# A four-layer graph network on one core: layer 2 back to plain tile order, and one layer turned on TensorE

## The chip, the core and the metric

The kernel runs on one core of a Trainium2 chip. Its engines work side by side and are ordered by semaphores: TensorE (PE) multiplies and transposes into the eight PSUM banks, VectorE (DVE) and ScalarE (ACT) do the elementwise work and empty the banks, GpSimd (POOL) takes small elementwise jobs, SyncE (SP) issues every DMA. The metric is the device time of one execution in microseconds (us).

## The reference, cut to what matters

A batch of 64 graphs of 256 nodes with 256 features goes through four layers, each with a normalisation without weights in front and a residual sum behind it:

```
h = relu(layernorm(x)); x = x + layer0(h, adj)   # attention, 8 heads: softmax over masked scores
h = relu(layernorm(x)); x = x + layer1(h, adj)   # additive attention, softmax over axis 1, elu
h = relu(layernorm(x)); x = x + layer2(h, adj)   # gated graph network, 3 rounds
h = relu(layernorm(x)); x = x + layer3(h, adj)   # additive attention, 4 heads
```

Layer 2 repeats three times, with the state `h` starting as its input:

```
m = h @ weight[i]; aggr = A.T @ m               # A = (adj != 0)
gi = aggr @ w_ih.T + b_ih; gh = h @ w_hh.T + b_hh
r, z = sigmoid(gi_r + gh_r), sigmoid(gi_z + gh_z)
n = tanh(gi_n + r * gh_n); h = (1 - z) * n + z * h
```

Layer 3 needs, per head, softmax over the keys of `leaky_relu(s_src + s_dst)` where the adjacency is 1, times the projected features.

## The kernel before, in words

Two graphs make a pair; 32 pairs pass through the four layers. A pair is a tile `x` of 128 partitions by four token groups (`t` 0 to 3, `T` = 4) of 256 features. Work tiles (`w4`, 29 slots of 128 x 1024 fp32) are shared by all pairs in flight; at most five pairs are (`x` has five slots).

*The plan.* Nothing is issued where the code stands. `add` (lines 73 to 109) records each task with its engine or engines (`forms`), its assumed duration and what it reads and writes. `order` (111 to 184) then simulates all engines and picks, again and again, the task and form that can begin first; ties go to the lower key, which is the pair's rank times `PERIOD` plus an offset per layer: `ON_PE` for TensorE, `ON_SP` for SyncE, `OTHERS` for the rest (lines 60 to 63). `MARGIN` is added in front of a DMA issue, `BACK` is a handicap for an engine of a task that could go elsewhere, and `RANKS` (1242) sets when the weights of layers 1 to 3 are prepared. Each engine, and SyncE as the queue of all DMAs, then runs its instructions in that fixed order.

*Normalisation* (`norm_relu_T`, 495 to 572). VectorE takes the statistics (L502, L504), GpSimd the power -0.5 of the variance (L516, L517). In layers 0, 1 and 3 VectorE scales each token group (L537), TensorE transposes the tile in eight 128 x 128 blocks (L555), and the two banks are emptied with the Relu (L567). Layer 2 needs its input in both forms, token by token (`xn`) and turned (`hT`). There the shift is worked out first (L523), ScalarE applies scale, shift and Relu (L532), and in all pairs but the last the tile is turned through DRAM.

*Turning through DRAM* (`through_dram`, 613 to 623). VectorE transposes 32 x 32 blocks, one DMA writes the tile to DRAM (L616), four read it back so that whole blocks change places (L619): five issues on SyncE. `turn` (625) does this for the attention tiles of layers 0 and 3 (L627), `turn_chunks` (630) for layer 2, in two half-tile transposes (L636). A tile from `turn_chunks` is *mixed*: node, then feature half, then token group, so that neighbours of one chunk lie eight elements apart. `chunk` (575) reads one chunk as weights, `wide` (582) a feature half as a moving operand.

*Layer 2* (`layer2`, 913 to 1154). Before the change `by_dma` (491) says that three tiles per pair go through DRAM: the normalised one and the states after rounds 0 and 1. Because the first is mixed, `woven` is set: the messages `aT` (evicted by L322, at 971) and the states `u` hold the four token groups of one node side by side, so chunks of them lie four elements apart. In rounds 0 and 1 the gates are products with the weights as the stationary and `hT` or `aT` as the moving operand, 512 columns wide (L988). In round 2 the tiles are the stationary operand, in chunks (L1084), for 512 columns (two gates) and for 256 (the new state). `messages` (943) splits the state into three bf16 parts, two of them remainders: the first subtraction (L946) also puts the token order right, the second is L951; 24 bf16 products per round (L965) multiply them by the adjacency mask.

*Layer 3* (`layer3`, 1156 to 1240). Prelu (L1191), mask and row minimum (`lowered`, L661), Exp (L669), the turn through DRAM (L627, L616, L619), products with the turned tile (L1213), transposes back (L1228), division (L1235), sum (L1240). In the last pair the normalisation in front is done in two halves (`fine`).

Of the kernel before, what the change touches and what calls it, by code (L numbers as in the profile page):

```python
# [16 lines left out]
P = 128  # L17
# [5 lines left out]
class Buf:  # L23


    def __init__(self, tag, tiles):
        self.tag, self.tiles, self.slot, self.parts = tag, tiles, None, {}
        self.fine = False
        self.woven = False
        self.mixed = False  # L30
# [9 lines left out]
class Plan:  # L40
# [15 lines left out]
    SLOW, MARGIN = 1.3, 0.6  # L56
    BACK = {"DVE": 1, "POOL": 1.1}


    PERIOD, REST = 133.7, 0  # L60
    ON_PE = (940, -967, 1371, -841)
    ON_SP = (1493, 2561, -1056, -1316)
    OTHERS = (1067, -773, -952, 397)
# [124 lines left out]
def tile_adj_preln_d4(  # L188
# [121 lines left out]
    def pool(n):  # L310
        return 0.16 + n / 460.0
# [14 lines left out]
    def either(do):  # L326

        return [(G, pool(N2), lambda: do(nc.gpsimd), True), (V, dve(N2), lambda: do(nc.vector), True)]
# [162 lines left out]
    def by_dma(what, p):  # L491

        return p < B // 2 - 1 and what in (2, (2, 0), (2, 1))

    def norm_relu_T(xt, p, tokens=False):
# [15 lines left out]
        xn, mixed, fine = w4(), by_dma(plan.layer, p), plan.layer == 3 and p == B // 2 - 1  # L511
        shift = tokens or mixed
        for ts in (slice(0, 2), slice(2, 4)) if fine else (slice(0, T),):
# [7 lines left out]
            if shift:  # L521
                add(
                    (V, 0.17, lambda: nc.vector.scalar_tensor_tensor(  # L523
                        rs()[:, 1, :], mv()[:, :, 0], -1.0, rs()[:, 0, :], ALU.mult, ALU.mult)),
                    reads=[mv], writes=[rs],
                )
        for g in range(2):

            def scaled(g=g):
                for t in (2 * g, 2 * g + 1):  # L530
                    if shift:
                        nc.scalar.activation(  # L532
                            tok(xn())[:, t, :], tok(xt())[:, t, :], AF.Relu,
                            bias=rs()[:, 1, t : t + 1], scale=rs()[:, 0, t : t + 1],
                        )
                    else:
                        nc.vector.tensor_scalar(  # L537
                            tok(xn())[:, t, :], tok(xt())[:, t, :], mv()[:, t, 0:1], rs()[:, 0, t : t + 1],
                            ALU.subtract, ALU.mult,
                        )  # L540

            add((A, 0.95, scaled) if shift else (V, 0.7, scaled, True), reads=[(xt, g), (mv, g), (rs, g)], writes=[(xn, g)])
        hT = w4()
        if mixed:
            turn_chunks(xn, "(t k b j)", hT)
            return (at, hT, xn) if tokens else (at, hT)
# [27 lines left out]

    def chunk(hT, k, t):
        if hT.mixed:
            return hT().rearrange("p (n x) -> p x n", x=2 * T)[:, T * k + t]
        if hT.woven:
            return tok(hT(), N2)[:, k].rearrange("p (n t) -> p t n", t=T)[:, t]
        return tok(hT(), N2)[:, k, t * P : (t + 1) * P]  # L580

    def wide(hT, k):

        if hT.mixed:
            return hT().rearrange("p (n k t) -> p k n t", k=2, t=T)[:, k]
        return tok(hT(), N2)[:, k]
# [43 lines left out]
    def turn_chunks(src, order, dst):  # L630

        e = w4()

        def blocks():
            for k in range(2):
                nc.vector.transpose(  # L636
                    e().rearrange("p (b i k t) -> p k b t i", b=4, i=32, k=2)[:, k],
                    src().rearrange(f"p {order} -> p k b t j", b=4, j=32, k=2)[:, k],
                )

        add((V, 2 * dve(N2), blocks), reads=[src], writes=[e])
        through_dram(e, dst)
        dst.mixed = True
# [13 lines left out]
    FUSED = 0.36  # L657
# [5 lines left out]
    def exp_rows(e, mn, zs, z0):  # L663


        def do():
            for r in range(4):
                row = rows_of(e())[:, r]
                nc.scalar.activation(  # L669
                    row, row, AF.Exp, bias=mn()[:, r : r + 1], scale=-1.0, accum_out=zs()[:, z0(r) : z0(r) + 1]  # L670
# [4 lines left out]
    def layer0(xt, p):  # L675
# [11 lines left out]
        for w, dst, nm in ((wq_sb, qT, "q"), (wk_sb, kT, "k")):  # L687
            for o in range(2):
                ps = bank()

                def product(w=w, o=o, ps=ps):
                    for k in range(2):
# [3 lines left out]
                by_node = lambda ap, hT=hT: ap.rearrange("p (t n) -> p n t", t=T) if hT.mixed else ap  # L696
                add(
                    evict(
                        N2, lambda dst=dst, o=o, f=by_node: f(tok(dst(), N2)[:, o, :]),
                        lambda ps=ps, hT=hT: tok(ps(), T) if hT.mixed else ps(),  # L700
                    ),
                    reads=[ps], writes=[(dst, o)],
                )
        for g in range(2):
            ps = bank()
            add((PE, 2.0 if hT.mixed else 1.74, lambda ps=ps, g=g: graph_mm(ps, hT, wv_sb, g)), reads=[hT, (QKV, 2)], writes=[ps], claims=[v])
# [3 lines left out]
        for g in range(2):  # L710
# [29 lines left out]
            for e, eT, mn in zip(es, pT, mns):  # L740
# [12 lines left out]
                for i in range(2):  # L753
# [3 lines left out]
                            (A, 2 * act(N, 1), lambda f=divided, rows=rows: f(nc.scalar.mul, rows)),  # L757
# [54 lines left out]
    def layer1(xt, p):  # L812
# [8 lines left out]
        for t in range(T):  # L821
# [6 lines left out]
            add((PE, 0.96 if hT.mixed else 0.89, product), reads=[hT, W1], writes=[ps], claims=[wh, f12])  # L828
# [29 lines left out]
        for g in range(2):  # L858
# [9 lines left out]
            def exp(g=g):  # L868
# [5 lines left out]
            add((V, 0.18, lambda two=two: nc.vector.reciprocal(rz()[:, two], zs()[:, two])), reads=[(zs, g)], writes=[(rz, g)])  # L874
            add(
                (V, dve(N2), lambda two=two: nc.vector.tensor_tensor(
# [422 lines left out]
```

## Time and profile before

| | us |
|---|---|
| median of 3 runs (3769.93 to 3773.58) | 3770.68 |
| profiled execution | 3770.94 |
| its span, first to last instruction | 3769.1 |
| TensorE busy | 3679.7 |
| VectorE busy | 3093.9 |
| ScalarE busy | 2521.8 |
| GpSimd busy | 594.1 |

A line of the profile names an engine, an operation, the tiles (out <- in), shapes and a count, and then durations. "Busy" is the union of the instructions' intervals. Matmuls overlap in their last part, so the spacing of their starts is their cost, and a busy TensorE may still hold short waits. `PEld` is the loading of a stationary operand, which runs beside the products. `w <- turn` is the way back from DRAM.

### The profile page before, as it was taken

How to read it: one execution, taken by the hardware profiler on the slowest of the kernel's cores; microseconds unless marked ns; L12 is line 12 of the kernel's file. 1: busy time of each engine (PE TensorE's matmuls, PEld its weight loads, DVE VectorE, ACT ScalarE, POOL GpSimd, SP SyncE). 2: the span in 40 equal slices, each digit the busy share in tenths (PEclk: the TensorE clock that was granted, in tenths of full speed). 3: DMA queues.
4: the chain of work that ended last, by engine and by line, in shares of the span. 5: the costliest groups of instructions: out<-in, count | busy, mean ns of one | idle time of the engine just before them, and what ended most of it. 6: DMA issues, size and time to landing. Idle time of an engine off the chain costs nothing.

```text
span 3769.1 us, 56446 instructions
## 1 busy us (share of the span) xinstructions
PE 3679.7 (98%) x17097; PEld 2308.8 (61%) x17097; DVE 3093.9 (82%) x7982; ACT 2521.8 (67%) x6756; POOL 594.1 (16%) x543
## 2 busy tenths in 40 slices
PE   7999999999999999999999999999999999999996
PEld 4556665666666666666666666666666666666663
DVE  7678779888888888888888888888888888888765
ACT  7776477776667776667776667776667776667544
POOL 2001111111112111111111111111121011121100
PEclk9999999999999999999999999999999999999997
DMA  8664367755566655566655566655666655666324
GB/s 235 171 196 129 105 195 199 201 163 169 164 184 201 183 170 169 162 191 197 188 166 168 162 191 199 187 166 165 170 188 196 188 165 165 171 194 185 115 79 129
DMA packets 469167, 651.88 MB, mean 173 GB/s; under 512 B 47744, under 2 KB 395264, under 8 KB 468864
## 3 DMA queue, kind: packets, MB, share of 16 engines
q1 hardware_dynamic: 468864, 648.28, 59.0%
q8 instruction: 137, 2.24, 0.2%
q14 instruction: 166, 1.36, 0.1%
HBM read 380.91 MB, written 267.19 MB: 172 GB/s over the span
## 4 chain that ended last, share of the span: by engine, by line
PE 29%; DVE 21%; ACT 14%; DMA 5%; issue 2%; SPq 2%; POOL 1%; POOLq 0%; DVEq 0%; ACTq 0%
PE ps L988 11%; ACT w L669 5%; PE ps L1084 5%; DMA w<-turn 5%; DVE st L502 3%; DVE w L537 3%; PE ps L1166 2%; PE ps L965 2%; ACT w L1191 2%; PE ps L592 2%; DVE w L627 2%; DVE w L636 2%; DVE w L1146 1%; SPq L619 1%; PE ps L720 1%
## 5 line engine op out<-in xcount | busy, mean ns | idle before, releaser
L669 ACT ACTIVATE w<-w,mx 128x256 f32<-128x256 f32 x1536 | 762.5, 508 | 36.0 <-DVE mx L661 35.8
L988 PE MATMUL ps<-w,whhT 128*128 128x512 f32 x1536 | 728.6, 601 | 3.8 <-DMA w<-turn 3.6
L988 PE MATMUL ps<-w,giT 128*128 128x512 f32 x1536 | 708.9, 593 | 0.2 <-ACT w L322 0.2
L322 ACT COPY w<-ps 128x512 f32<-128x512 f32 x518 | 386.3, 765 | 344.6 <-PE ps L592 151.8
L627 DVE STREAM_TRANSPOSE w<-w 128x1024 f32<-128x1024 f32 x384 | 473.1, 1238 | 104.3 <-ACT w L669 55.3
L988 PEld LDWEIGHTS ps<-w,giT 128*128 128x128 f32 x1536 | 288.9, 190 | 351.2 <-issue 331.9
L988 PEld LDWEIGHTS ps<-w,whhT 128*128 128x128 f32 x1536 | 276.8, 191 | 301.9 <-issue 282.6
L661 DVE CUSTOM_DVE_ANT_0 w<-ps,mask 128x256 f32<-128x256 f32 x1024 | 368.6, 417 | 44.1 <-PE ps L720 42.8
L751 ACT ACTIVATE w<-w,rz 128x256 f32<-128x256 f32 x910 | 387.9, 505 | 5.0 <-DVE rz L744 3.4
L1084 PE MATMUL ps<-whhT,w 128*128 128x512 f32 (+1 forms) x1024 | 375.6, 504 | 0.1
L1084 PE MATMUL ps<-giT,w 128*128 128x512 f32 (+1 forms) x1024 | 364.3, 494 | 0.0
L1084 PEld LDWEIGHTS ps<-giT,w 128*128 128x128 f32 x1024 | 281.7, 312 | 74.5 <-issue 5.1
L1084 PEld LDWEIGHTS ps<-whhT,w 128*128 128x128 f32 x1024 | 274.5, 317 | 64.2 <-issue 14.8
L669 ACT ACTIVATION_READ_ACCUMULATOR w<-w,mx 128x1 f32 x1536 | 309.4, 201 | 0.0
L1031 POOL TENSOR_TENSOR w<-w,w 128x512 f32<-128x512 f32 x91 | 121.7, 1338 | 1168.8 <-ACT w L1026 1077.8
L965 PE MATMUL ps<-mask,w 128*128 128x256 bf16 x2304 | 272.0, 274 | 4.0 <-DVE mask L917 2.9
L965 PEld LDWEIGHTS <-w 128*128 128x128 bf16 x2304 | 231.3, 108 | 70.9 <-issue 45.7
L661 DVE CUSTOM_DVE_ANT_0 w<-w,mask 128x256 f32<-128x256 f32 x512 | 201.5, 425 | 29.7 <-ACT w L1191 29.7
L1191 ACT ACTIVATE w<-w,f 128x256 f32<-128x256 f32 x512 | 219.2, 511 | 0.0
L1117 ACT ACTIVATE w<-w 128x512 f32<-128x512 f32 x128 | 80.2, 627 | 192.0 <-DVE w L1113 190.9
L636 DVE STREAM_TRANSPOSE w<-w 128x512 f32<-128x512 f32 x186 | 197.3, 1122 | 10.6 <-ACT w L532 10.6
L537 DVE TENSOR_SCALAR w<-x,mv,rs 128x256 f32<-128x256 f32 x384 | 165.7, 484 | 47.9 <-POOL rs L517 47.9
(124 smaller groups left out, 5853.6 us busy)
## 6 DMA issues: line engine op xcount, KB each, us to landing
turn<-w SPq DMA_DIRECT2D x477, 512.0 KB, 3.0
w<-turn SPq DMA_DIRECT2D x1908, 128.0 KB, 3.7
w<-in_adj_dram SPq DMA_DIRECT2D x128, 512.0 KB, 5.2
w<-row SPq DMA_DIRECT2D x64, 512.0 KB, 4.9
x<-in_x_dram SPq DMA_DIRECT2D x64, 256.0 KB, 5.2
out_dram<-x SPq DMA_DIRECT2D x64, 256.0 KB, 4.5
w<-row SPq DMA_DIRECT2D x32, 256.0 KB, 3.1
w<-in_L_gnn_weight_dram SPq DMA_DIRECT2D x3, 256.0 KB, 7.6
```

Source lines behind the costliest of these rows:

```text
L322: (A, act(n), lambda: nc.scalar.copy(dst(), src())),
L537: nc.vector.tensor_scalar(tok(xn())[:, t, :], tok(xt())[:, t, :], mv()[:, t, 0:1], rs()[:, 0, t : t + 1], ALU.subtract, ALU.mult,)
L627: add((V, dve(T * N), lambda: nc.vector.transpose(blocks(), blocks())), writes=[e])
L636: nc.vector.transpose(e().rearrange("p (b i k t) -> p k b t i", b=4, i=32, k=2)[:, k], src().rearrange(f"p {order} -> p k b t j", b=4, j=3 ...
L661: nc.vector.tensor_tensor_reduce(row, src, mask, scale, 3.0e38, ALU.add, ALU.min, mn)
L669: nc.scalar.activation(row, row, AF.Exp, bias=mn()[:, r : r + 1], scale=-1.0, accum_out=zs()[:, z0(r) : z0(r) + 1])
L751: op(row, row, rz()[:, r : r + 1])
L965: mm(ps()[:, g * N : (g + 1) * N], chunk_of(part(), part.mixed, t, o), tok(am(), N)[:, t, :], start=i == 0 and c == 0, stop=i == 2 and c == 1,
L988: mm(ps(), w[:, k, c0 : c0 + P], wide(src, k), start=n == 0, stop=n == 2 * len(terms) - 1)
L1031: either(lambda eng, o=o, u=u, hT=hT, hn=hn: eng.tensor_sub(*((tok(at_o(u, o), T), wide(hT, o), tok(at_o(hn, o), T)) if hT.mixed else (at_ ...
L1084: mm(out, chunk(src, k, t), w[:, k, c0 : c0 + n], start=m == 0, stop=m == 2 * len(terms) - 1)
L1191: (A, act(N, 1), lambda t=t, g=g, h=h, e=e, r=r: nc.scalar.activation(rows_of(e())[:, r].rearrange("p b (c j) -> p c b j", c=2), sd[g]().r ...
```

## The change

1. Layer 2's normalised tile is turned by TensorE in every pair, as in the other layers; `by_dma` now only sends the states after rounds 0 and 1 through DRAM, as tokens `h`. `woven` is gone: `hT`, `aT` and `u` are plain, and evictions, `chunk` and `wide` are simple. Tiles from `turn_chunks` stay mixed and come from one whole-tile VectorE transpose.
2. In `messages` both remainders keep the order of `h`, so where `h` is mixed all three parts are read as weights eight elements apart.
3. Normalisation may run on VectorE or on ScalarE in layers 0, 1 and 3, and layer 1's division as well; the shift is worked out for every tile.
4. Layer 3 of the last pair: the four tiles are kept in row order and turned by TensorE (`turn_keys`, eight transposes and two evictions each) instead of through DRAM; the mask is one instruction.
5. The planner's constants and some assumed durations differ.

```
-    SLOW, MARGIN = 1.3, 0.6
-    BACK = {"DVE": 1, "POOL": 1.1}
-    PERIOD, REST = 133.7, 0
-    ON_PE = (940, -967, 1371, -841)
-    ON_SP = (1493, 2561, -1056, -1316)
-    OTHERS = (1067, -773, -952, 397)
+    SLOW, MARGIN = 1.3, 0.2
+    BACK = {"DVE": 0.8, "POOL": 1.3}
+    PERIOD, REST = 260.1, 0
+    ON_PE = (128, 788, 5100, -4300)
+    ON_SP = (3449, 2192, 2058, -4527)
+    OTHERS = (100, -16, -1143, 1788)
...
-    def by_dma(what, p):
-        return p < B // 2 - 1 and what in (2, (2, 0), (2, 1))
+    def by_dma(l, p):
+        return p < B // 2 - 1
...
-            add((A, 0.95, scaled) if shift else (V, 0.7, scaled, True), reads=[(xt, g), (mv, g), (rs, g)], writes=[(xn, g)])
+            if tokens:
+                forms = (A, 1.0, lambda f=scaled: f(AF.Relu))
+            else:
+                forms = [(V, 0.7, scaled_v, True), (A, 1.0, lambda f=scaled: f(AF.Identity))]
+            add(forms, reads=[(xt, g), (mv, g), (rs, g)], writes=[(xn, g)])
         hT = w4()
-        if mixed:
-            turn_chunks(xn, "(t k b j)", hT)
-            return (at, hT, xn) if tokens else (at, hT)
...
+    def turn_keys(e, eT):
+        for c in range(2):
+            ps = bank()
+            def product(c=c, ps=ps):
+                for r in range(4):
+                    nc.tensor.transpose(ps()[:, r * P : (r + 1) * P], tok(e(), N)[:, r, c * P : (c + 1) * P], ident)
+            add((PE, 4 * TURN, product), reads=[e], writes=[ps], claims=[eT])
+            add(evict(N2, lambda c=c: eT()[:, c * N2 : (c + 1) * N2], ps), reads=[ps], writes=[(eT, c)])
...
-        def blocks():
-            for k in range(2):
-                nc.vector.transpose(
-                    e().rearrange("p (b i k t) -> p k b t i", b=4, i=32, k=2)[:, k],
-                    src().rearrange(f"p {order} -> p k b t j", b=4, j=32, k=2)[:, k],
-                )
-        add((V, 2 * dve(N2), blocks), reads=[src], writes=[e])
+        add(
+            (V, dve(T * N) + 0.04, lambda: nc.vector.transpose(
+                e().rearrange("p (b i x) -> p b x i", b=4, i=32), src().rearrange("p (x b j) -> p b x j", b=4, j=32))),
+            reads=[src], writes=[e],
+        )
...
-                    in_order(rest[0](), False), in_order(h(), h.mixed), in_order(upper(h()), h.mixed), ALU.subtract), True),
+                    rest[0](), h(), upper(h()), ALU.subtract), True),
...
-                    ps()[:, g * N : (g + 1) * N], chunk_of(part(), part.mixed, t, o), tok(am(), N)[:, t, :],
+                    ps()[:, g * N : (g + 1) * N], chunk_of(part(), h.mixed, t, o), tok(am(), N)[:, t, :],
...
-                    evict(N2, lambda o=o: messages_out(aT, o), lambda ps=ps: tok(ps(), P) if woven else ps()),
+                    evict(N2, lambda o=o: at_o(aT, o), ps),
...
-                turn(e, eT[k])
+                if last:
+                    turn_keys(e, eT[k])
+                else:
+                    turn(e, eT[k])
...
-    RANKS = (1.4, 1.1, 1)
+    RANKS = (1.7, 2.3, 1.2)
```

## The prediction

> **What bounds the kernel now.** I read the page first, then the busy times in stretches of the span, then TensorE's waits, then its order of work, and the end of the run last. The page's first two parts:
>
> ```profile
> span 3769.1 us, 56446 instructions
> PE 3679.7 (98%) x17097; PEld 2308.8 (61%) x17097; DVE 3093.9 (82%) x7982; ACT 2521.8 (67%) x6756; POOL 594.1 (16%) x543
> PE   7999999999999999999999999999999999999996
> PEclk9999999999999999999999999999999999999997
> ```
>
> TensorE is busy nearly all the time at nearly full clock; VectorE, at 82%, is the next. Four stretches show where TensorE is not full:
>
> ```profile
> core 0: us, PE busy (x) PEld busy (x) DVE busy (x) ACT busy (x) POOL busy (x), PEclk, DMA share, GB/s
> 0.00:400.00 400.00, 362.26 (x1796) 225.03 (x1798) 301.39 (x859) 275.19 (x764) 50.72 (x57) 0.95 0.64 185
> 400.00:3500.00 3100.00, 3084.94 (x14419) 1943.53 (x14420) 2615.90 (x6752) 2120.90 (x5684) 518.24 (x462) 1.00 0.61 177
> 3500.00:3700.00 200.00, 193.85 (x734) 119.24 (x733) 137.08 (x270) 97.38 (x221) 19.46 (x17) 0.99 0.29 90
> 3700.00:3769.00 69.00, 38.67 (x153) 21.00 (x151) 39.57 (x102) 28.37 (x88) 5.66 (x7) 0.73 0.56 157
> ```
>
> Of some 89 us without TensorE work, 38 lie in the first 400 us, 15 in the long middle, 36 in the last 270. So two things can move the time: TensorE's own work per pair of graphs, and the two ends. TensorE's waits over the whole run:
>
> ```profile
> PE ps L1213 <- DMA w<-turn: 19.7, 2, 15.0
> PE ps L555 <- DVE w L537: 16.8, 25, 7.3
> PE ps L988 <- DMA w<-turn: 3.6, 1, 3.6
> ```
>
> The first is the end of the last pair's layer 3; the second is the transposes of a normalised tile behind VectorE's normalisation; the third is the only wait for a tile that layer 2 turned through DRAM. TensorE's order in the middle:
>
> ```profile
> 1532.46 1.89 PE L592 MATMUL ps<-wo_sb,w 128*128 128x256 f32 x8
> 1534.18 2.03 PE L1084 MATMUL ps<-giT,w 128*128 128x256 f32 x8
> 1536.05 1.90 PE L1084 MATMUL ps<-whhT,w 128*128 128x512 f32 x4
> ...
> 1552.00 0.38 PE L555 MATMUL ps<-ident,w 128*128 128x128 f32 x2
> 1552.57 1.09 PE L555 MATMUL ps<-ident,w 128*128 128x128 f32 x6 [0.18 <-DVE w L537]
> 1553.49 1.88 PE L988 MATMUL ps<-w,whhT 128*128 128x512 f32 x4
> ...
> 1560.36 1.04 PE L555 MATMUL ps<-ident,w 128*128 128x128 f32 x8
> 1561.23 1.88 PE L693 MATMUL ps<-w,wk_sb 128*128 128x512 f32 x4
> 1562.95 3.65 PE L826 MATMUL ps<-w1a,w 128*128 128x258 f32 x16
> 1566.44 1.54 PE L555 MATMUL ps<-ident,w 128*128 128x128 f32 x8
> 1567.82 0.27 PE L795 MATMUL ps<-ident,f 128*4 128x128 f32 x1
> ```
>
> Matmuls are pipelined, so the cost is from one start to the next line's start. Eight 256-column products from a plain tile (L592) take 1534.18 - 1532.46 = 1.72 us; eight from the interleaved tiles of layer 2 (L1084) take 1.87. Eight transposes take 0.87 undisturbed (1560.36 to 1561.23), but 1.49 and 1.38 where VectorE is late.
>
> **The change, term by term.** The sum is made against the profiled execution, 3770.9 us (span 3769.1 and 1.8 around it), 0.2 above the median.
>
> *Transposes added.* Layer 2's normalised tile is turned by 8 transposes in 31 of the 32 pairs: 31 x 0.87 = +27.0 us. In the middle TensorE has no hole to put them in, so they count in full. The Trainium skill (TensorE: Matmul & The Clock Gate, Part 4) gives some 275 ns for a transpose inside a kernel; this speaks against the change, since 248 of them would be 68 us and the sum below would end some 30 us slower than before. The trace shows where that figure lies: a transpose's record here is 273 ns at the median, but the next starts 109 ns later, so I go by the spacing.
>
> *A wait in front of them.* The three such groups of one pair are stretched by 0.62, 0 and 0.51 us, 0.38 in the mean. The new ones wait for four ScalarE normalisations (587 ns each). 31 x 0.38 = +12; the ends are 0 and 0.62 x 31 = +19. Matmuls queued behind them wait too, and nothing overtakes.
>
> *Interleaved weight loads removed.* In the middle L1084 loads its weights in 308 to 328 ns; in the last pair, whose tiles are plain, the same line needs 190. Against 512 columns (429 ns) both hide; against 256 they don't: 0.15 us per group of 8, to two decimals, and 0.14 by the single starts. 31 pairs x 4 groups x 0.14 = -17.4. The first 512-column product behind a group that splits the array's rows is up to 0.23 us longer, once a pair; I take half, -3.6. Together -21, ends -17 and -25.
>
> *Loads newly interleaved.* In messages the two remainder tiles now keep the order in which the tokens landed: 32 more interleaved bf16 loads per pair, 992 in all. Before, 16 per pair are so: 142 to 148 ns against 98, and the next matmul still starts 109 ns later. So 0, with 992 x 36 ns = +36 as the other end, if a run of them could not overlap as the present two in a row do.
>
> *VectorE.* It loses 186 half-tile block transposes (L636, 197 us). For the 62 whole-tile ones I take twice the 1.06 us that one of L636 costs (197.3 / 186), since its output is spaced in the same way (L627, fully plain, has 1.24): 131. The remainder's subtraction (L946) falls from 2.01 to 1.22 in 62 cases: -50. The shift of the mean (178 ns) comes to 97 more tiles: +17. Net some -99 us, under 3 points of its 84% in the middle. ScalarE loses 186 spaced copies of 1.09 us for plain ones of 0.58 (-95) and may get 62 new ones (+36). None of this bounds the run, but it is what TensorE waits for at L555: 1.13 us a pair, 36 in the run. I take 15 of these off; the ends are 0 (the wait is one of order and not of load) and -36.
>
> *DMA.* 31 round trips fall away, 155 issues on SyncE and 32 MB of 652. Only the 3.6 us wait of the first pairs goes: -4. Without that cover, the path would have cost some 12 us of latency a pair; deeper buffers hide it in the middle.
>
> *Last pair's layer 3.* The end of the run:
>
> ```profile
> 3748.91 1.25 DVE L627 STREAM_TRANSPOSE w<-w 128x1024 f32<-128x1024 f32 x1 [0.72 <-ACT w L669]
> 3750.57 6.05 SPq L619 DMA_DIRECT2D w<-turn  x12
> 3755.97 1.98 PE L1213 MATMUL ps<-w,f 128*64 128x256 f32 x8 [4.63 <-DMA w<-turn]
> 3759.66 3.48 PE L1213 MATMUL ps<-w,f 128*64 128x256 f32 x16
> 3765.25 0.69 DVE L1240 TENSOR_TENSOR x<-w,x 128x512 f32<-128x512 f32 x1
> ```
>
> The last exponential ends at 3748.88 and the last L1240 at 3765.94. With transposes: two groups of four (0.9), an eviction (0.6), the second half of L1213 (2.0, cold), copy 0.6, L1228 1.0, L1235 and L1240 0.7 each: 3755.4, so -10. If the eight evictions fall to ScalarE, whose 16 us of Prelu and Exp end this path, 5 of it is lost again: -5. If TensorE stays warm the products halve: -13.
>
> *The plan's constants.* Offsets, period, margin and ranks change the order everywhere; no row prices this. Bounds: the 36 us without work at the end and the 38 at the start could be halved (-35), or as much added (+35). I take 0, because both sets of offsets put TensorE's layer 2 last.
>
> Sum: 27 + 12 - 21 + 0 - 15 - 4 - 10 = -11, so 3770.9 - 11 = 3760 us. The measurement tells some 0.2% (7.5 us) from no change; this is just beyond it.
>
> **Rivals.**
> - *No relief (same).* L555's waits come from order: the -15 goes, and the sum is +4: 3775. For it: in the middle VectorE is only 84% busy.
> - *Order gains (faster).* The ends lose 30 us of their 74: 3730. For it: TensorE's clock is 0.95 in the first 400 us and 0.73 in the last 69, so less idling there would pay twice. Against: the last pair's chain after its layer 2 (from 3716) is latency.
> - *The new transposes stall TensorE (slower).* The four normalisations that feed them wait for the tile's statistics and GpSimd's power (1.04 us), and the DMA path had room for that. The planner books 1.0 us for two that take 1.17. At 1.5 us per pair instead of 0.38 the price is 31 x 1.12 = +35: 3795. Break-even is 0.38 + 11/31 = 0.73 us per pair. For it: ScalarE itself idled 93.5 us in front of these activations.
> - *Interleaved bf16 loads bind (slower).* +36: 3796; it decides from 11 us, 11 ns per load. The Trainium skill (SBUF — State Buffer, Door 1: The DMA port swizzle) says that every access which enters a new 16-byte line pays, and these take 32 bytes a step. The 144 ns against 98 agree; the unchanged 109 ns spacing says that two in a row hide it, and 24 in a row are not shown.
> - *Plain tiles don't help (slower by 10).* The last pair's 190 ns speaks against it.
>
> **How the numbers follow.** Forecast 0.36; order gains 0.16; no relief 0.15; stalls 0.20; bf16 loads 0.08; the last 0.05. Faster is 0.36 + 0.16 = 0.52, same 0.15, slower 0.33. The forecast's own range, by its terms' ends taken together without the constants, is 3740 to 3775 (all good ends at once are no likelier than all bad ones). The whole reaches from just below the order's gain, 3728, to just above the two slower cases, 3800; some 1 in 10 is left out on either side.
>
> **What would show it.** Right: L1084's loads at 190 ns and eight 256-column products in 1.73 us; 1,024 transposes of normalised tiles (776 before) at 109 ns spacing, with waits in front of the new groups below 0.5 us; L965 still at 109 ns; L322 near 0.58 us; VectorE below 3,000 us busy; no 15 us wait at L1213 at the end. Wrong: waits of L555 for ScalarE that sum to more than 25 us, L965 above 115 ns, or a middle stretch below 99% TensorE.

## The result, and the profile after

The changed kernel takes 3718.39 us (median of 4, 3717.08 to 3718.92) against 3770.30 (3769.26 to 3773.58) beside it: 0.986 of the time, 95% interval 0.9843 to 0.9877. That is 52 us faster, where 10 were forecast and the range began at 3728. Lines of the code have moved: L988 of before is L971, L965 is L949, L1084 is L1066, L555 is L553, L532 is L528, L322 is L321, L1213 is L1211; in layer 3 L669 (Exp) is L666, L1228 is L1227 and L1240 is L1239. L627, a block transpose before, is now a transpose of `turn_keys`.

The page of the changed kernel, its first two parts:

```profile
span 3715.3 us, 56987 instructions
PE 3657.9 (98%) x17377; PEld 2186.9 (59%) x17377; DVE 2881.1 (78%) x7648; ACT 2693.9 (73%) x7227; POOL 532.9 (14%) x494
PE   8999999999999999999999999999999999999997
PEclk8999999999999999999999999999999999999998
```

TensorE has 280 products more and is busy 22 us less; VectorE loses 213 us, ScalarE gains 172. The same four stretches, the last two set 50 us earlier because the run ends earlier:

```profile
core 0: us, PE busy (x) PEld busy (x) DVE busy (x) ACT busy (x) POOL busy (x), PEclk, DMA share, GB/s
0.00:400.00 400.00, 377.33 (x1934) 230.85 (x1935) 297.53 (x881) 299.59 (x832) 49.81 (x59) 0.97 0.64 181
400.00:3450.00 3050.00, 3036.47 (x14481) 1814.69 (x14480) 2414.88 (x6389) 2259.82 (x6062) 466.94 (x417) 1.00 0.60 170
3450.00:3650.00 200.00, 197.82 (x777) 115.55 (x775) 130.96 (x273) 97.72 (x227) 13.01 (x13) 0.99 0.30 91
3650.00:3715.00 65.00, 46.26 (x191) 25.82 (x189) 37.69 (x109) 36.76 (x109) 3.15 (x5) 0.81 0.35 106
```

TensorE is without work for 22.7 us of the first 400 (37.7 before), for 13.5 in the middle (15.1), for 21 at the end (36). TensorE's waits, the largest four:

```profile
PE ps L553 <- ACT w L528: 12.7, 17, 7.9
PE ps L842 <- DVE mask L806: 9.8, 13, 1.0
PE ps L356 <- ACT w L321: 6.6, 1, 6.6
PE ps L627 <- ACT w L666: 6.3, 6, 3.2
```

The 15 us wait for the turned tile at the end is gone; the transposes of normalised tiles now wait for ScalarE, 7.9 of the 12.7 us in one place (L842 turns a mask in layer 1, L356 turns weights at the start). TensorE's order in the middle:

```profile
1516.52 2.79 PE L949 MATMUL ps<-mask,w 128*128 128x256 bf16 x24
1519.14 3.60 PE L971 MATMUL ps<-w,whhT 128*128 128x512 f32 x8
...
1530.58 1.88 PE L971 MATMUL ps<-w,giT 128*128 128x512 f32 x4
1532.29 1.04 PE L553 MATMUL ps<-ident,w 128*128 128x128 f32 x8
1533.17 1.89 PE L582 MATMUL ps<-wo_sb,w 128*128 128x256 f32 x8
```

From start to start: 24 bf16 products take 2.62 us (109 ns each), eight transposes 0.88. The loads behind two of these lines, from 600 to 3340 us (count, then minimum, median and maximum in ns):

```profile
L949 PEld LDWEIGHTS <-w x1752: 97/143/168, 611.9 to 3331.2; 128*128 128x128 bf16 x195
...
L1066 PEld LDWEIGHTS ps<-giT,w x780: 189/190/193, 601.3 to 3321.1; 128*128 128x128 f32 x195
```

L1066 is down from 308 to 328 ns, as said. The bf16 loads are at 143 ns, longer than the 109 ns from product to product, and 24 in a row leave that spacing as it was.

**Where the 52 us lie.** The loads of `x` on SyncE mark the pairs. At the start of the run five pairs are in flight, so the sixth pair's load shows when the pipeline is full, and the last pair's when it begins to empty. In the queue of the kernel before, and then of the changed one, the sixth pair's load; below it, the first and the last of the 64 loads (two to a pair, so the last one is the second half of the last pair; its first half is issued at 3347.1 us before and at 3324.6 in the changed kernel):

```profile
408.93 2.04 SPq L1248 DMA_DIRECT2D x<-in_x_dram  x2
...
L1248 SPq DMA_DIRECT2D x<-in_x_dram x64: 373/468/1467, 0.7 to 3348.4; - x64
```

```profile
386.11 0.94 SPq L1247 DMA_DIRECT2D x<-in_x_dram  x2
...
L1247 SPq DMA_DIRECT2D x<-in_x_dram x64: 413/467/1175, 0.7 to 3325.0; - x64
```

The start is 22.8 us shorter, the 26 pairs in between take 113.01 and 113.02 us each, and what lies behind the last pair's first load falls from 422.0 to 390.7, by 31.3. So the middle came out as the sum had it (nearly nothing), but by other terms, as shown below: that is in part luck. The gain is in the ends, where the forecast had 14 (10 for layer 3 of the last pair, 4 for the first pairs' wait).

The same from TensorE's side. Each product is given the spacing to the next start that its shape has when nothing disturbs it (0.43 us for 512 columns, 0.216 for 256, 0.109 for a transpose, and so on); what its start-to-start time has above that counts as lost. It includes waits too short to leave a hole between two pipelined records.

| us | work at full spacing | lost to 400 | 400 to 3340 | after 3340 |
|---|---|---|---|---|
| before | 3538.4 | 63.3 | 102.0 | 58.2 |
| changed | 3568.9 | 35.0 | 65.1 | 38.3 |

TensorE got 30.5 us more to do and loses 85 us less. The middle loses 37 us less too, just enough to pay for the transposes.

### The profile page after: what moved, and what is told of

Same layout as the page of the kernel before. It is cut to its first block, busy times and chain, and to the rows that moved or that the text cites. A ratio compares the mean times of both kernels' runs of the same rounds, so it can differ in the third digit from the quotient of the medians.

```text
span 3715.3 us, 56987 instructions
## 1 busy us (share of the span) xinstructions
PE 3657.9 (98%) x17377; PEld 2186.9 (59%) x17377; DVE 2881.1 (78%) x7648; ACT 2693.9 (73%) x7227; POOL 532.9 (14%) x494
## 4 chain that ended last, share of the span: by engine, by line
PE 72%; ACT 13%; DVE 7%; DMA 5%; issue 1%; SPq 1%; POOL 0%; DVEq 0%; POOLq 0%; ACTq 0%
PE ps L971 24%; PE ps L1066 14%; ACT w L666 6%; PE ps L690 6%; PE ps L582 5%; PE ps L949 4%; PE ps L1159 3%; PE ps L553 3%; PE ps L883 3%; PE ps L710 2%; ACT w L741 2%; DMA w<-turn 2%; PE ps L760 2%; PE ps L1211 2%; PE ps L816 2%; DMA turn<-w 1%
## 5 line engine op out<-in xcount | busy, mean ns | idle before, releaser
L666 ACT ACTIVATE w<-w,mx 128x256 f32<-128x256 f32 x1536 | 758.7, 498 | 15.9 <-DVE mx L659 14.3
L971 PE MATMUL ps<-w,whhT 128*128 128x512 f32 x1536 | 722.1, 596 | 0.7 <-DVE w L1031 0.5
L971 PE MATMUL ps<-w,giT 128*128 128x512 f32 x1536 | 715.1, 594 | 0.0
L321 ACT COPY w<-ps 128x512 f32<-128x512 f32 (+1 forms) x564 | 318.9, 582 | 313.4 <-PE ps L690 99.8
L971 PEld LDWEIGHTS ps<-w,giT 128*128 128x128 f32 x1536 | 288.5, 190 | 337.8 <-issue 326.2
L971 PEld LDWEIGHTS ps<-w,whhT 128*128 128x128 f32 x1536 | 277.5, 190 | 279.2 <-issue 256.2
L1066 PE MATMUL ps<-whhT,w 128*128 128x512 f32 (+1 forms) x1024 | 363.6, 491 | 0.0
L1066 PE MATMUL ps<-giT,w 128*128 128x512 f32 (+1 forms) x1024 | 356.1, 486 | 0.0
L528 ACT ACTIVATE w<-x,rs 128x256 f32<-128x256 f32 x472 | 247.5, 591 | 96.4 <-DVE rs L520 92.6
L666 ACT ACTIVATION_READ_ACCUMULATOR w<-w,mx 128x1 f32 x1536 | 292.3, 190 | 0.0
L1066 PEld LDWEIGHTS ps<-giT,w 128*128 128x128 f32 x1024 | 193.5, 190 | 149.0 <-issue 134.7
L659 DVE CUSTOM_DVE_ANT_0 w<-w,mask 128x256 f32<-128x256 f32 x512 | 200.5, 417 | 102.1 <-ACT w L1189 102.0
L949 PEld LDWEIGHTS <-w 128*128 128x128 bf16 x2304 | 243.5, 128 | 52.0 <-issue 32.8
L949 PE MATMUL ps<-mask,w 128*128 128x256 bf16 x2304 | 272.5, 274 | 0.0
L1066 PEld LDWEIGHTS ps<-whhT,w 128*128 128x128 f32 x1024 | 189.8, 191 | 116.0 <-issue 99.5
L514 POOL TENSOR_SCALAR rs<-mv 128x4 f32<-128x4 f32 x129 | 55.7, 432 | 1180.0 <-DVE mv L503 1131.9
L501 DVE BATCH_NORM_STATS2 st<-x 128x6 f32<-128x256 f32 x512 | 190.9, 415 | 41.4 <-DMA x<-in_x_dram 38.3
```

What stands on the lines that cost most here:

```text
L321: (A, act(n), lambda: nc.scalar.copy(dst(), src())),
L501: nc.vector.bn_stats(st()[:, t, :], tok(xt())[:, t, :])
L528: nc.scalar.activation(tok(xn())[:, t, :], tok(xt())[:, t, :], func, bias=rs()[:, 1, t : t + 1], scale=rs()[:, 0, t : t + 1])
L659: nc.vector.tensor_tensor_reduce(row, src, mask, scale, 3.0e38, ALU.add, ALU.min, mn)
L666: nc.scalar.activation(row(e, r), row(e, r), AF.Exp, bias=mn()[:, r : r + 1], scale=-1.0, accum_out=zs()[:, z0(r) : z0(r) + 1])
L949: mm(ps()[:, g * N : (g + 1) * N], chunk_of(part(), h.mixed, t, o), tok(am(), N)[:, t, :], start=i == 0 and c == 0, stop=i == 2 and c == 1,)
```

## The experiments

The kernel's own planner (`order`) yields a time for every instruction, so its end and its stages can be set beside the chip's. These are not measurements, but the distance between plan and chip turned out to be the key. Here for the kernels of this section (start, to the sixth load; per pair, mean of 26; end, behind the last pair's load):

| us | plan: start, per pair, end | plan's end | chip: start, per pair, end | span |
|---|---|---|---|---|
| before | 395.6, 110.39, 426.6 | 3692 | 408.9, 113.01, 422.0 | 3769 |
| changed | 379.3, 111.96, 392.8 | 3683 | 386.1, 113.02, 390.7 | 3715 |
| changed, old constants | 387.8, 112.62, 437.2 | 3753 | 391.0, 113.71, 435.4 | 3783 |
| before, new constants | 400.3, 112.41, 384.9 | 3708 | 410.7, 116.26, 379.0 | 3812 |
| before, prices corrected | 403.5, 112.30, 434.5 | 3758 | 405.5, 112.46, 425.1 | 3754 |
| before, corrected, planned anew | 389.7, 111.81, 426.8 | 3724 | 390.7, 112.14, 413.7 | 3720 |

**Are the constants the gain?** The first pair of runs swaps all of them (`SLOW` to `OTHERS`, `RANKS`) between the kernels:

```
-    SLOW, MARGIN = 1.3, 0.2
-    BACK = {"DVE": 0.8, "POOL": 1.3}
-    PERIOD, REST = 260.1, 0
-    ON_PE = (128, 788, 5100, -4300)
...
+    SLOW, MARGIN = 1.3, 0.6
+    BACK = {"DVE": 1, "POOL": 1.1}
+    PERIOD, REST = 133.7, 0
+    ON_PE = (940, -967, 1371, -841)
...
```

> The changed kernel with all planner constants of before (period, offsets, margin, handicaps, ranks). Constants theory: the 23 us won before the first pair leaves and most of the 31 us won behind the last load come from the constants, so this run lands near 3755 us (3745 to 3770), its first output near 405 us. Work theory: the ends were won by the changed work itself (layer 2's tile without the way through DRAM, layer 3 of the last pair on TensorE, normalisation on ScalarE), so this run stays within 10 us of the changed kernel, 3710 to 3730.

> The kernel before with all planner constants of the changed one. Constants theory: it gains most of the ends, 3725 to 3745 us. Work theory: it stays within 10 us of before, 3760 to 3780. If constants only suit the kernel they were chosen for, it is slower than before, over 3780.

Measured: 3784.69 (ratio 1.0041, 1.0026 to 1.0055) for the changed kernel with the old constants, and 3814.7 (1.0124, 1.0109 to 1.0139) for the kernel before with the new ones. Either is worse than both originals. The first lies above the ranges of both its theories; of the second's three cases the last one came. In sum the new constants are worth 66 us to the changed kernel and cost the other 45. The pairs' loads, of the changed kernel with the old constants and of the kernel before with the new ones, divide that by stages:

```profile
391.04 0.94 SPq L1247 DMA_DIRECT2D x<-in_x_dram  x2
...
3347.56 0.43 SPq L1247 DMA_DIRECT2D x<-in_x_dram  x1
```

```profile
410.72 0.52 SPq L1248 DMA_DIRECT2D x<-in_x_dram  x1
...
3433.44 1.09 SPq L1248 DMA_DIRECT2D x<-in_x_dram  x2
```

With the table above, the two ends come apart. The sixth load moves with the tasks (and the prices that go with them): the changed ones bring it 17.9 us earlier under the old constants and 24.6 under the new, while the constants alone move it by +1.8 and −4.9. What lies behind the last load moves with the constants: the new ones shorten it by 43.0 us with the tasks of before and by 44.7 with the changed ones, while the changed tasks alone make it 13.4 and 11.7 longer. In the middle the two can't be told apart: there the new constants cost the kernel before 84 us and save the changed one 18. So the constants suit one task list each in the middle, and carry the gain at the end of the run. (These are single profiled executions; two of the changed kernel differ by 1.6 us at the start and 0.5 at the end.)

**Layer 3 of the last pair.** `last = hT.fine` becomes `last = False`, so that it goes through DRAM again.

> The changed kernel with the last pair's layer 3 turned through DRAM again. By the prediction's own term this costs 10 us (5 to 13): 3728. Constants theory: the same 10, since the term is apart from the order. If the tail was won mostly by this edit, it costs 20 to 30: 3738 to 3748.

Measured: 3716.76 (3712.07 to 3718.67; ratio 0.986, 0.9846 to 0.9875), no different from the changed kernel: neither the 10 us of the prediction nor the 20 to 30 came. The end of the changed kernel's run, and then that of this one:

```profile
3705.25 0.76 PE L627 MATMUL ps<-ident,w 128*128 128x128 f32 x5 [0.16 <-ACT w L666]
3705.61 1.07 ACT L321 COPY w<-ps 128x512 f32<-128x512 f32 x2 [0.42 <-PE ps L627]
...
3710.00 0.69 DVE L1239 TENSOR_TENSOR x<-w,x 128x512 f32<-128x512 f32 x1
```

```profile
3696.40 0.49 ACT L666 ACTIVATE w<-w,mx 128x256 f32<-128x256 f32 x1
...
3697.44 1.97 PE L1211 MATMUL ps<-w,f 128*64 128x256 f32 x8 [14.60 <-DMA w<-turn]
...
3710.74 0.69 DVE L1239 TENSOR_TENSOR x<-w,x 128x512 f32<-128x512 f32 x1
```

On TensorE the last sum starts 4.9 us after the last exponential (3705.1), through DRAM 13.9 after (3696.9): 9 us are saved there. But between its Prelu and Exp ScalarE now empties banks (L321), and from the first full run of Prelu (3686.66 and 3683.04) to the last exponential it takes 18.4 us instead of 13.9. That gives back half. The remaining 3.6 us were lost before: the changed kernel's last layer starts so much later. Why is not settled.

**Either-engine normalisation.** The `(A, …)` forms of the normalisation in layers 0, 1 and 3 and of layer 1's division are taken out:

```
-                forms = [(V, 0.7, scaled_v, True), (A, 1.0, lambda f=scaled: f(AF.Identity))]
+                forms = [(V, 0.7, scaled_v, True)]
...
-                    (A, 2 * act(N, 1), divided),
```

> The changed kernel with normalisation of layers 0, 1 and 3 and layer 1's division on VectorE alone. If moving them to ScalarE removed the waits at the transposes of the normalised tiles, some 15 us come back: 3733 and more time lost per pair at those transposes; if these waits are hidden by the pair's fixed rhythm, within 5 us of 3718.

Measured: 3752.0 (0.9956, 0.9942 to 0.9971), 34 us above the changed kernel. But its constants were again those of another task list, so a later run plans the same kernel anew (other constants, and the price of L636 corrected to 1.95):

> The changed kernel with normalisation and division on VectorE alone, the transposes' price put right, and constants moved to suit (the plan's own end is 3705 us: 381 to the sixth load, 112.1 per pair, 408 behind the last). Plan theory: the 34 us that taking ScalarE's form away cost under the old constants was mostly a misfit of constants; 387 + 2927 + 407 = 3721 in the span, 3715 to 3730. If a second engine for the normalisation is worth 34 us by itself, 3745 to 3755.

Measured: 3724.21 (0.9877, 0.9864 to 0.9891), beside the changed kernel at 3716.05 on the same chip. That is 8 us. Beside the changed kernel with the same price corrected and constants chosen anew (3709.57 on that chip, the last experiment below) it is 15. So of the 34 us some 8 to 15 belong to the choice of engine, as far as each set of constants is equally good, and the rest to constants that no longer fit.

**The price of the transposes.** Layer 2's eight are issued twice:

```
-                for j, (k, t) in enumerate(chunks):
+                for j, (k, t) in [*enumerate(chunks)] * (2 if tokens else 1):
```

> The changed kernel in its own order with layer 2's eight transposes issued twice over. If TensorE's work counts in full, as the term for the transposes has it: +27 to +28 us, 3746, nearly all in the middle. If the transposes lie in waits of TensorE, less than 10.

Measured: 3741.45 (0.9923, 0.9908 to 0.9937), 23 us above the changed kernel for 256 transposes more (all 32 pairs), 90 ns each; the 26 middle pairs take 113.78 us each, 0.76 more, or 95 ns for each. TensorE stays busy and at full clock:

```profile
400.00:3340.00 2940.00, 2928.38 (x14037) 1754.63 (x14036) 2313.88 (x6122) 2175.59 (x5823) 446.91 (x400) 1.00 0.59 168
```

So 27 us was right in kind, and the 275 ns per transpose of the Trainium skill (TensorE: Matmul & The Clock Gate, Part 4), by which the 248 of the change would be an estimated 68, is not what a transpose costs here: the fp32 transposes' records do last 273 ns, but overlap. (The page measured bf16 transposes.)

**What the interleaved tiles cost, in the order of before.** The next four leave the kernel before and its order as they are, and only read or write parts of layer 2 as if they were plain, so that tokens are mixed up but the amount of work stays the same. First the weight loads (in `chunk`), then all of it, then the eviction of the messages alone, then the remainder's subtraction alone:

```
-        if hT.woven:
-            return tok(hT(), N2)[:, k].rearrange("p (n t) -> p t n", t=T)[:, t]
```
```
-                    evict(N2, lambda o=o: messages_out(aT, o), lambda ps=ps: tok(ps(), P) if woven else ps()),
+                    evict(N2, lambda o=o: messages_out(aT, o), ps),     # messages_out returns at_o(aT, o)
```
```
-            if mixed:
-                return ap.rearrange("p (m k t) -> p t k m", k=2, t=T)   # in in_order
```

> The kernel before, in its own order, but round 2 of layer 2 reads its stationary chunks as if the tiles were plain (wrong numbers, same amount of work). By the prediction's term this takes 21 us (17 to 25) off: 3749. If TensorE's order holds waits that take up what a shorter product frees, less: 3755 to 3768.

> As the run with plain chunks, and the messages' eviction and the remainder's subtraction read and write plainly too (wrong numbers); the normalised tile still goes through DRAM and the order is that of before. Plan theory (the ends are as long as the order makes them, the middle as long as TensorE's work and its waits): head and tail stay near 409 and 422 us, the middle falls from 113.0 to about 111.5 us per pair: 3725 to 3740, all of it from the middle. Work theory: head and tail fall too, by 15 us or more each.

> The kernel before, in its own order, with only the messages' eviction written plainly (wrong numbers): 186 ScalarE copies of 0.58 us in place of 1.09. The run with everything plain gave 58 us, plain chunks alone 5. If the products behind the messages waited for these copies, most of the other 53 comes here: 3725 to 3740. If VectorE's late normalisation is what holds TensorE, 3755 to 3770.

> The kernel before, in its own order, with only the remainder's subtraction reading plainly (wrong numbers): 62 VectorE instructions of 1.22 us in place of 2.01, 50 us less on VectorE. If VectorE's queue is what holds TensorE, most of the 53 us comes here: 3720 to 3740. If ScalarE's copies are, 3755 to 3770.

| made plain | us | ratio, interval | against before |
|---|---|---|---|
| weight loads | 3766.29 | 0.9991, 0.9981 to 1.0 | −5 |
| eviction of the messages | 3731.64 | 0.9898, 0.9885 to 0.9912 | −38 |
| remainder's subtraction | 3758.91 | 0.9972, 0.9961 to 0.9983 | −11 |
| all three | 3712.79 | 0.9847, 0.983 to 0.9863 | −58 |

The parts add up to 54 of the 58. The weight loads' 5 us, where 21 were expected, are at the edge of what can be told from nothing. With all three plain, 48 of the 58 lie in the middle (111.15 us per pair), 6 at the start and 3 at the end. What the freed loads did is seen in the idle time of the weight loads in front of the norm transposes (L555, 600 to 3340 us; us and times), in the kernel before, with plain loads, and with the plain eviction:

```profile
  DVE w L537: 42.8, 166
```

```profile
  DVE w L537: 59.9, 172
```

```profile
  DVE w L537: 16.0, 68
```

With plain loads TensorE is busy 23 us less (3656.4), as the term had it, and then waits longer for the same normalisation. The plain eviction took 27 of the 43 us of that wait away, though it is on ScalarE and the normalisation on VectorE: the two hand work to each other in a fixed order, and what is longer than planned can make all behind it late. How much longer can be read in the kernel before, from the groups by shape (busy us and mean ns of one; L322 mixes plain evictions of 0.58 us and 185 interleaved ones) and, on the timeline, from one eviction, one subtraction and one pair of half-tile transposes to what follows on the engine:

```profile
L322 ACT COPY w<-ps 128x512 f32<-128x512 f32 x516 | 385.8, 767 | 344.6 <-PE ps L592 151.8 <-PE ps L693 129.0 <-PE ps L1213 25.9
L636 DVE STREAM_TRANSPOSE w<-w 128x512 f32<-128x512 f32 x186 | 197.3, 1122 | 10.6 <-ACT w L532 10.6
...
1521.59 1.10 ACT L322 COPY w<-ps 128x512 f32<-128x512 f32 x1
1522.45 0.92 ACT L751 ACTIVATE w<-w,rz 128x256 f32<-128x256 f32 x2
...
1509.87 2.03 DVE L946 TENSOR_TENSOR w<-w 128x1024 f32<-128x1024 f32 x1 [0.20 <-DMA w<-turn]
1511.83 0.67 DVE L1022 TENSOR_TENSOR w<-ps,w 128x512 f32<-128x512 f32 x1
...
1536.43 2.04 DVE L636 STREAM_TRANSPOSE w<-w 128x512 f32<-128x512 f32 x2 [0.29 <-ACT w L532]
1538.33 0.67 DVE L1129 SCALAR_TENSOR_TENSOR w<-w,ps 128x512 f32<-128x512 f32 x1
```

The plan counts from one start to the next, which is shorter than a record: a plain eviction lasts 0.58 us, the next instruction starts 0.46 later at the earliest, and the plan books 0.48 (`act(512)`). For the interleaved one it books the same 0.48, where the next start comes 0.86 later; 1.13 for the subtraction (`dve(1024)`), where it comes 1.96 later; and 1.20 for the two half-tile transposes, where it comes 1.90 later. Over 185, 62 and 93 cases that is some 70 us of ScalarE and 51 + 65 us of VectorE that the plan does not know of. The changed kernel has no such eviction and a plain subtraction; one price is still short, 1.17 for L636, whose records last 2.03 us and whose next start comes 1.85 later at the earliest:

```profile
L321 ACT COPY w<-ps 128x512 f32<-128x512 f32 x563 | 318.6, 582 | 313.4 <-PE ps L690 99.8 <-PE ps L949 80.5 <-PE ps L760 57.3
...
L636 DVE STREAM_TRANSPOSE w<-w 128x1024 f32<-128x1024 f32 x62 | 126.1, 2034 | 0.1
```

That the interleaved forms are dearer agrees with the Trainium skill (SBUF — State Buffer, Door 1: The DMA port swizzle: an access that enters a new 16-byte line pays); the page prices none of them.

**Is it the plain tiles, or a plan that fits?** The interleaved tiles stay, and the planner of the kernel before is told what they take, first with its constants as they were, then with constants chosen for it (not printed: four prices that differ by 0.01 to 0.4 us):

```
-        add((V, 2 * dve(N2), blocks), reads=[src], writes=[e])
+        add((V, 2.0, blocks), reads=[src], writes=[e])
...
-                (V, dve(T * N), lambda: nc.vector.tensor_tensor(
+                (V, 1.95 if h.mixed else dve(T * N), lambda: nc.vector.tensor_tensor(
...
-                    evict(N2, lambda o=o: messages_out(aT, o), lambda ps=ps: tok(ps(), P) if woven else ps()),
+                    [(f[0], 0.92, f[2]) for f in evict(...)] if woven else evict(N2, ..., ps),
...
-            add((PE, 1.74, product), reads=[src, HH, GI[l]], writes=[ps], claims=claims)
+            add((PE, 1.88 if woven else 1.74, product), reads=[src, HH, GI[l]], writes=[ps], claims=claims)
```
```
+    SLOW, MARGIN = 1.3, 0.47
+    BACK = {"DVE": 1.0, "POOL": 1.02}
+    PERIOD, REST = 139.5, 0
+    ON_PE = (940, -910, 1371, -841)
+    ON_SP = (1420, 2308, -1229, -1316)
+    OTHERS = (753, -847, -683, 538)
...
+    RANKS = (1.4, 1.05, 1)
```

> The kernel before with the planner's prices put to what its trace shows and its own constants. The plan's own end is 3758 us (403 to the sixth load, 112.3 per pair, 435 behind the last load). Plan theory: right prices alone don't help without constants that suit them, since the ends come out as planned: 3760 to 3780. If wrong prices alone cost the time, as good as with moved constants: 3722 to 3735.

> The kernel before with the planner's prices put to what its trace shows (half-tile transposes 2.0 us, spaced eviction 0.92, reordering subtraction 1.95, 256-column products from interleaved tiles 1.88) and its constants moved a little to suit; no other change. The plan's own end for it is 3724 us, with 390 us to the sixth pair's load, 111.8 per pair, and 427 behind the last load. Plan theory: head and tail come out within 8 us of that (395, 427), the middle near 113: 3755 to 3762. If the tiles' form itself costs the time and the order does not, no change: 3765 to 3775.

Measured: 3756.0 (0.9961, 0.9947 to 0.9975) and 3722.17 (0.9869, 0.9855 to 0.9884). Right prices alone bring 14 us, which lies between the two cases expected; constants chosen for them bring another 34, far below the 3755 to 3762 expected, since the middle came out as planned (112.14 us per pair) and not near 113. With right prices the plan's end and the chip's span lie 3 us apart, under either set of constants; with the old prices, the kernel before ends 77 and 105 us behind its plan. So its distance from the plan goes with the prices and not with the constants. (The changed kernel ends 32 and 30 behind under the two sets.) And the kernel before, with every interleaved tile and every trip through DRAM, is then within 4 us of the changed one, its weight loads as busy as ever:

```profile
PE 3646.6 (98%) x17097; PEld 2303.0 (62%) x17097; DVE 3033.7 (82%) x7927; ACT 2552.2 (69%) x6784; POOL 702.9 (19%) x570
```

It gets there another way: 22 us in the middle, 18 at the start, 8 at the end. A rival is left: no run chooses constants anew under the old prices, so that the 34 us need the right prices is not shown.

**A version that beats both.** The changed kernel with its one short price put right (`dve(T * N) + 0.04` to 1.95) and constants chosen again: `BACK` of POOL 1.26, `ON_PE` (7, 389, 5100, −4300), `ON_SP`'s last −4509, `OTHERS` (−44, −16, −1143, 1841).

> The changed kernel with one more price put right (its whole-tile transposes last 1.9 us between starts, planned 1.17) and four constants moved to suit: the plan's own end is 3691 us (383 to the sixth load, 112.7 per pair, 377 behind the last load). Plan theory: the ends as planned, the middle at 113: 387 + 2938 + 378 = 3703 in the span, 3706 us, 12 faster than the changed kernel. If the tail does not come out as planned, no faster than 3718.

> The changed kernel once more, as the yardstick beside the two others: 3718 us, ratio 0.986.

> The replanned changed kernel again, on the same chip as the changed kernel. If the 9 us between the two earlier were real, 3709 against 3718 here too; if they came from different chips, less than 4 apart.

Measured: 3709.67 (3704.74 to 3712.2; 0.9837, 0.9823 to 0.985) where 3706 was expected, and again, beside the changed kernel: 3709.57 (3707.05 to 3712.54; 0.9838, 0.9824 to 0.9851) against 3716.05 (3714.73 to 3718.64; 0.9857, 0.9843 to 0.987). The times of the two do not overlap, though the intervals of their ratios to the kernel before just do: some 6 us, the best version here. It still ends 20 us behind its plan (3691 for a span of 3711), and why is open.

This is also the fairer comparison of the two kernels. With the short prices put right and constants chosen anew on both sides, the changed one takes 3709.57 us and the one before 3722.17: 12.6 us apart, and the intervals (0.9824 to 0.9851, 0.9855 to 0.9884) do not meet. That both searches for constants went equally far is not shown.

## Why the prediction was right and wrong

The sign was right, and the sum of the middle; the size was a fifth of what came, and what came lies at the ends, mostly behind the last load, where the constants carry it. By its terms:

- *Transposes added, +27*: right. Doubling them (256 more) costs 23.
- *A wait in front of them, +12*: too high. The excess in front of and between the transposes of normalised tiles, from 600 to 3340 us, is 8.8 us in 97 groups, 0.09 each; before it was 26.8 in 72, 0.37 each. (A transpose behind a product that splits the array starts 304 to 311 ns after it in 36 of 37 cases; that is not counted as a wait.) New and old groups now wait less.
- *Interleaved weight loads, −21*: the loads fell as said, and alone they take 23 us off TensorE's busy time, but only 5 off the run. TensorE spent the rest waiting, 17 us of it at L555.
- *Loads newly interleaved, 0*: right; the +36 end is out, since 24 in a row still start 109 ns apart.
- *VectorE and ScalarE, −15*: the term that was mis-sized in the middle. I took 15 of the 36 us by which the transposes at L555 were late, with all 36 as the end, for VectorE's and ScalarE's work together. The eviction and the subtraction alone were worth 49 in the order of before, beyond that end. With the plain eviction the groups at L555 lose 9.6 us in place of 26.8 (600 to 3340 us), less than half of the 38 that the run won; the rest lies in waits that the term left out. The list of waits, with 16.8 us at L555 in the whole run, shows even less: a wait shorter than the overlap of two pipelined records leaves no gap between them. ScalarE also got 172 us busier where I had it lose 59: 344 of 384 normalisations of layers 0, 1 and 3 went to it (472 at L528, 128 of them layer 2's).
- *DMA, −4*: the wait is gone from the list; too small to be told apart.
- *Last pair's layer 3, −10*: failed. Within that layer the forecast's own low end (−5, if the evictions fall to ScalarE) came true, but in the time nothing is left of it, since the layer starts 3.6 us later; why is open.
- *The plan's constants, "I take 0"*: the step that failed. Put back to those of before, they cost the changed kernel 66 us, twice the bound of 35: 45 of it behind the last load, 18 in the middle, 5 at the start. The argument, that both sets put TensorE's layer 2 last, says nothing of how pairs overlap at the ends. The plan's own stages, which need no run, had −16 at the start and −34 at the end; the chip gave −23 and −31. In the middle the plan had 1.57 us more per pair, the chip none, because the kernel before fell 2.6 us per pair behind its plan and the changed one 1.1.

Of the rivals, *order gains* (3730, 0.16) comes nearest: without work at the ends TensorE now has 44 us of 74, the 30 that it named. But the two ends are 54 us shorter, and at the start the tasks gave more than the constants. *New transposes stall* and *interleaved bf16 loads bind* are refuted by the numbers above, while *plain tiles don't help* is half right: the loads did fall to 190 ns, but that is worth 5 us, and it is the plain eviction and subtraction that help. Each sign of a right step did appear, and none of the wrong ones (TensorE's waits for ScalarE at the norm transposes are 12.7 us, counted as the 16.8 before was); they tested the middle, while the gain lay elsewhere.

What is shown: the kernel before ran an order made with prices too short for its interleaved tiles; making these operations plain in that order gives 58 us, putting the prices right gives 14, and with constants chosen anew 49. At the end of the run the gain comes with the constants, at the start with the tasks. What stays open is a division of the 52 among the other four parts of the change: in the middle each set of constants fits one task list, so a part taken out under fixed constants (34 us for the normalisation) measures the misfit more than the part. The 12.6 us that are left with both kernels planned anew are close to the 11 forecast with the constants at 0; since its terms were off in both directions, that is no proof of them.

## What to carry to other kernels

Where the order is written out ahead of time, hold every duration it assumes against the trace first, from start to start; an operation that takes far longer than its price can make what is behind it late, on other engines too, and the plan's end far below the measured span was the sign of it here. Changing layout and constants together hides which of the two helped: correct the prices and plan anew on both sides before a layout gets the credit (here some 13 us of the 52 were left). When TensorE is 98% busy, count its start-to-start time against the undisturbed spacing, since waits shorter than the overlap of its records leave no gap between them.

## What the runs showed of the hardware that was not expected

- An interleaved output or input makes the record of an elementwise pass 1.6 to 1.9 times as long: the eviction of 128 x 512 fp32 with 16 bytes between neighbours takes 1.10 us against 0.58 on ScalarE, the subtraction of 128 x 1024 with 32 bytes between its inputs 2.01 against 1.23 on VectorE, the block transpose with 32 bytes between its outputs 2.03 against 1.24.
- The bf16 loads at 32 bytes a step take 143 ns, longer than the 109 ns between their products, and with 24 in a row the products still start 109 ns apart.
- 256 more transposes cost 23 us, 90 ns each, and the granted clock stays at 1.00 in the middle.
